# Key and query convolutions of an attention block by Strassen–Winograd products taken twice instead of once

## The chip, the cores and the metric

The kernel runs on one core of a Trainium2 chip. TensorE (PE) multiplies, VectorE (DVE), ScalarE (ACT) and GpSimd (POOL) do elementwise work, and SyncE (SP) issues nearly all DMAs. The metric is the device time of one execution in microseconds; lower is better. Everything is fp32.

## What is computed

Eight images of 512 channels and 32 x 32 = 1024 tokens pass through two attention blocks. Block 0 has a group norm of 32 groups and eight heads of 64 channels; block 1 has a group norm of 8 groups and one head of 512 channels. Cut to what matters here, block 0 is:

```python
h = group_norm(x, gn_weight, gn_bias)                       # 32 groups
qkv = einsum('oc,bct->bot', w_qkv, h) + b_qkv[None, :, None]
qkv = qkv.reshape(B * nh, 3 * C // nh, T)
q, k, v = qkv[:, :ch], qkv[:, ch:2 * ch], qkv[:, 2 * ch:]
weight = softmax(einsum('bct,bcs->bts', q * scale, k * scale))
a = einsum('bts,bcs->bct', weight, v)
out = x + einsum('oc,bct->bot', w_proj, a) + b_proj[None, :, None]
```

The change concerns the q and k of block 0: two products of a 512 x 512 matrix with the 512 x 1024 image. A bias of k adds the same number to all scores of a query, so the softmax doesn't depend on it.

## The kernel before

**One level of seven products.** Each convolution splits the weights and the image in 2 x 2 halves and makes seven products of half size in place of eight (`wino`, L226). Sums of the weights' quarters (factors 5, 6, 3, 7) are made once and kept in DRAM (`prepare`, `keep`); a convolution loads all seven factors, 1.79 MB, with `load_weight` (L298) into a pool of three tiles. The list `uses` fixes the order of these loads, and a load is issued when a convolution ends. The sums of the image's quarters (`image_factors`, L311) are 16 VectorE operations of 512 columns per image, each reading two SBUF operands.

`wino` does a product per step, on two output tiles i of 128 x 512 each. Product 1 goes to bank a, is copied by ScalarE (t1) and continued by product 2 in a. Products 6, 7 and 4 add up in bank b; product 5 and 3 in bank c. Between two of them VectorE reads the partial sum (`upper`, `done`): u2 = b + t1 after 6, u3 = b + t1 after 7, the output quarters from c and b. The last two steps stand in a list `tail`; `finish()` runs them after step 1 of the following convolution, so that there is always a product between a bank's reading and its next writing.

**Order.** TensorE's instructions, some of ScalarE's and some of VectorE's are kept in program order (`keep_in_program_order`); for the rest a scheduler orders each engine by priority. `background` is a list of small jobs (image factors, statistics of the next norm), of which each step runs some. `hooks` are jobs tied to a step.

**An image.** Attention of block 0 for image b (`attention0`, L400) has eight blocks of scores: eight tiles sc of 128 x 1024 in three PSUM tiles, ScalarE's e = exp(sc), VectorE's sums of the e, then av, the product with v. `reciprocals` (L371) takes the sums; the result is multiplied in by GpSimd. Then come block 1 of image b - 1 (`layer1_scores`, `layer1_rest`), the projection, and the convolutions for image b + 1: `queries` (q), then `keys_and_values` (k, then v). Scores of b + 1 follow directly after v. The norm of image b + 2 is made within these convolutions: statistics on VectorE from four loads `ahead`, `group_mean` (L109: one small matmul, four VectorE operations of four columns) and `affine` (L122: a small matmul, VectorE's ve, GpSimd's power rstd at L127, then VectorE's s, ms and b). `biased` (L351) writes q and k with their bias added: ScalarE for the quarter from bank a, VectorE for the others.

The prologue does the same for image 0 with the sums fresh in SBUF, and forms m (the product of block 1's query and key weights), z (of its value and projection weights) and the bias rows.

Of the kernel before, what the change touches and what calls it, by code (L numbers as in the profile page):

```python
# [9 lines left out]
F32 = mybir.dt.float32  # L10
# [4 lines left out]

P = 128
EPS = 1e-5
NBIG = 32


# [8 lines left out]
def two_attention_blocks_kernel(  # L29
# [41 lines left out]
    def pcols(name):  # L71
        i = 4 * PARAMS.index(name)
        return par[:, i : i + 4]
# [101 lines left out]
    def main_path(ctx):  # L175
# [46 lines left out]
        def finish():  # L222
            while tail:
                tail.pop(0)()
# [46 lines left out]
        wdram = {n: dram.tile([P, 7, 2, C // 2], F32, name=f"sums_{n}") for n in weights}  # L271

        def weight_factors(t):
            return {p: t[:, p - 1, :, :] for p in range(1, 8)}

        def prepare(n):
            t = wpool.tile([P, 7, 2, C // 2], F32, tag="w", name=f"prepare_{n}")
# [11 lines left out]
        def keep(n, t):  # L289
            nc.sync.dma_start(wdram[n], t)  # L290

        uses = ["q", "p", "k", "v"] if B > 1 else ["p"]
        for b in range(1, B):
            uses += ["m", "p", "z"] + (["q", "k", "v"] if b + 1 < B else [])
        uses += ["m", "z"]
        loaded = []

        def load_weight():  # L298
            if uses:
                n = uses.pop(0)  # L300
                t = wpool.tile([P, 7, 2, C // 2], F32, tag="w", name=f"w_{n}_{len(uses)}")
                nc.sync.dma_start(t, wdram[n])
                loaded.append((n, t))

        def weight(n):
            name, t = loaded.pop(0)
            assert name == n
            return weight_factors(t)


        def image_factors(h, uid):  # L311
# [53 lines left out]
        def conv(wf, hf, bias, name, **kw):  # L365
            out = channel_tiles(name)
            by_channel(wf, hf, name, biased(out, bias), **kw)
            return out


# [204 lines left out]
        def prologue():  # L575
            raw_k = raw("k", 5)
            raw_q = raw("q", 4)
            h0 = [load_x(0, c, "h0") for c in range(KC)]
            first = {n: prepare(n) for n in "vqk"}
            wk = natural(raw_k, "k", ("a", "b"))  # L580
            wq = natural(raw_q, "q", ("c", "acc"))
            norm = GroupNorm(0, "0_0", pinned=True)
            for c in range(KC):
                norm.stats(c, h0[c])
            hf, steps = image_factors(h0, "h0_0")

# [23 lines left out]
            q = conv(weight_factors(first["q"][0]), hf, pcols("bq0"), "q0_0")  # L610
            k = conv(weight_factors(first["k"][0]), hf, pcols("bk0"), "k0_0")
# [12 lines left out]
            later.append([  # L624
                lambda: tc.keep_in_program_order(nc.vector.tensor_copy(ubias, bias[0])),
                lambda: tc.keep_in_program_order(nc.vector.tensor_add(obias[1], bias[1], pcols("bp1"))),
                lambda: tc.keep_in_program_order(nc.vector.tensor_add(obias[0], bias[2], pcols("bp0"))),
            ])
            return v, q, k, norm1, later
# [56 lines left out]
                [lambda: norm.affine(acc_tile(f"gvar_{uid}")[:, :KC])],  # L686
            ]

        def keys_and_values(b, hf, hooks):

            norm = None
            if b + 1 < B:
                norm = GroupNorm(0, f"0_{b + 1}")
                for c in range(KC):
                    background.append(lambda c=c: norm.stats(c, load_x(b + 1, c, "ahead")))
            k = conv(weight("k"), hf, pcols("bk0"), f"k0_{b}", hooks=hooks, after=[load_weight])
            hooks = [[all_background], [], [], [], []]
            if norm:
                hooks[1].append(lambda: norm.group_mean(acc_tile(f"gmean_0_{b + 1}")[:, :KC]))
                hooks[3].append(lambda: norm.affine(acc_tile(f"gvar_0_{b + 1}")[:, :KC]))  # L700
            v = by_token(weight("v"), hf, f"v0_{b}", hooks=hooks, after=[load_weight])
            return k, v, norm

        def queries(b, h, hooks=()):
            hf, steps = image_factors(h, f"h0_{b}")
            background.extend(steps)
            q = conv(
                weight("q"), hf, pcols("bq0"), f"q0_{b}", middle=(2, 5, 6, 7), hooks=hooks, back=4, after=[load_weight],
            )
            return hf, q  # L710

        def layer1_scores(b, h, hooks):
            hf, steps = image_factors(h, f"h1_{b}")
# [34 lines left out]
        for b in range(B):  # L748
            extra = [[] for _ in range(2 * 2 * KC)]
            for i, fs in enumerate(later):  # L750
                extra[i] += fs
            later = []
            h, loads, applies = [], [], []
            if b > 0:
                h, loads, applies = begun(load_again, norm1, b - 1, "h1")
            elif B > 1:
                h, loads, applies = begun(load_x, norm0, 1, "h0")
            for f in loads:
                f()
            for i, f in enumerate(applies):  # L760
                extra[2 * i + 3].append(f)
            psum_pools(f"attention_{b}", 1)
            a, scaled = attention0(b, q, k, v, extra)
            psum_pools(f"products_{b}", 2)
            xt = [load_x(b, c, "x") for c in range(KC)]
            af, ends = attention_steps(a, scaled, b)
            if b > 0:
                hf, gf = layer1_scores(b - 1, h, ends)
                norm1 = projection(b, af, xt)
                if b + 1 < B:  # L770
                    h, loads, applies = begun(load_x, norm0, b + 1, "h0")
# [220 lines left out]
```

## Time and profile before

| what | value |
|---|---|
| median of 3 runs | 2933.57 us (2933.5 to 2934.69) |
| profiled execution | 2936.12 us, span 2934.3, TensorE clock 0.999 |
| DMA | 245.80 MB, mean 84 GB/s |
| VectorE adds of 128x512 from PSUM (w_k, L237) | 692 ns each, x16 |
| ScalarE's exponentials (e, L417) | 476.0 us, x512, mean 1050 ns |
| ScalarE's copies from PSUM, 128x512 (L248) | 586 ns each |
| GpSimd's multiplications a<-a,r (L438) | 104.0 us, x56 |

One profiled execution: times are microseconds from the start of the span unless marked ns. A row names line, engine, operation, output<-inputs and their shapes, count, busy time and mean. "Idle before" is the engine's own waiting time ahead of an instruction, and the arrow names what ended it. PEld is TensorE's weight load, which runs beside its products. A matmul of fp32 has two MATMUL records.

In the timeline of before, the convolutions for image 2 lie at 610 to 697 us: q, from 641 k, from 665 v; the scores begin at 696.6.

### The profile page before, as it was taken

To read this page: it belongs to the slowest core of one execution; us is meant where nothing else is said; L and a number is where in the kernel's file an instruction comes from. 1 tells how busy PE (TensorE), PEld (TensorE's weight loads), DVE (VectorE), ACT (ScalarE), POOL (GpSimd) and SP (SyncE) were. 2 spreads that over 40 slices of the span, in tenths; PEclk is the share of its full clock that TensorE was granted. 3 is DMA by queue.
4 is the path that set the end of the run, shared out by engine and by line. 5 is a ranking of instruction groups with operands and counts; after the bars stand their busy time and mean duration, and the time that the engine had idled before them with its cause. 6 is when DMAs were issued, how large, how long until landed. Compare 5 with 4: busy or idle time off the path is not lost.

```text
span 2934.3 us, 26701 instructions
## 1 busy us (share of the span) xinstructions
PE 2919.7 (100%) x10250; PEld 1390.3 (47%) x10250; DVE 1852.9 (63%) x2381; ACT 809.3 (28%) x1005; POOL 201.7 (7%) x161
## 2 busy tenths in 40 slices
PE   9999999999999999999999999999999999999999
PEld 5434534545345453454534544345543455334544
DVE  5487577555876458664686546866477653776555
ACT  1251251213512035120451104411054110531110
POOL 0010010000100001000120001100011000110000
PEclk9999999999999999999999999999999999999999
DMA  7332302222032221222212221122311222112201
GB/s 264 131 128 107 119 19 103 78 106 87 23 108 97 76 86 48 83 97 75 90 46 81 97 100 66 48 79 104 122 39 45 79 108 90 40 44 79 90 4 66
DMA packets 69676, 245.80 MB, mean 84 GB/s; under 512 B 9955, under 2 KB 16931, under 8 KB 63014
## 3 DMA queue, kind: packets, MB, share of 16 engines
q1 hardware_dynamic: 69126, 243.87, 22.9%
q8 instruction: 82, 1.34, 0.2%
q14 instruction: 52, 0.43, 0.0%
q10 hardware_dynamic: 416, 0.16, 0.0%
HBM read 197.03 MB, written 46.96 MB: 83 GB/s over the span
## 4 chain that ended last, share of the span: by engine, by line
PE 98%; DVE 1%; DMA 0%; issue 0%; ACT 0%; SPq 0%; DVEq 0%
PE sc L66 15%; PE av L66 15%; PE psb_sc L66 6%; PE psb_av L66 6%; PE psa_av L66 4%; PE psa_sc L66 4%; PE psc_av L66 4%; PE psc_sc L66 4%; PE psb_z L66 3%; PE psb_g L66 3%; PE psb_k L66 3%; PE psb_p L66 3%; PE psb_v L66 3%; PE psb_q L66 3%; PE psa_g L66 2%; PE psa_v L66 2%
## 5 line engine op out<-in xcount | busy, mean ns | idle before, releaser
L421 DVE TENSOR_TENSOR sum<-sum,e 128x1024 f32<-128x1024 f32 x384 | 519.3, 1352 | 41.4 <-DVE sum L421 0.9
L417 ACT ACTIVATE e<-sc 128x1024 f32<-128x1024 f32 x512 | 476.0, 1050 | 164.6 <-PE sc L66 164.6
L66 PE MATMUL sc<-q,k 64*128 64x512 f32 x2048 | 456.8, 596 | 0.0
L66 PE MATMUL av<-e,v 128*64 128x512 f32 x2048 | 453.6, 595 | 0.0
L66 PEld LDWEIGHTS sc<-q,k 64*128 64x128 f32 x2048 | 190.4, 186 | 239.7 <-ACT e L417 119.2
L66 PEld LDWEIGHTS av<-e,v 128*64 128x64 f32 x2048 | 141.4, 137 | 304.3 <-issue 304.3
L382 DVE RECIPROCAL rc<-sums 128x256 f32<-128x256 f32 x72 | 126.4, 1756 | 87.7 <-PE sums L66 85.4
L384 POOL TENSOR_TENSOR all_recs<-all_recs,rc 128x256 f32<-128x256 f32 x72 | 63.8, 886 | 1056.9 <-DVE rc L382 1049.3
L435 ACT COPY a<-av 128x512 f32<-128x512 f32 x64 | 37.5, 586 | 321.3 <-PE av L66 321.3
L469 ACT ACTIVATE e<-e 128x512 f32<-128x512 f32 x96 | 60.5, 630 | 232.7 <-DVE e L468 232.7
L438 POOL TENSOR_TENSOR a<-a,r 128x512 f32<-128x512 f32 x56 | 104.0, 1857 | 276.1 <-DMA r<-rows 260.0
L419 DVE TENSOR_TENSOR sum<-e,e 128x1024 f32<-128x1024 f32 x64 | 78.6, 1227 | 60.1 <-ACT e L417 60.1
L66 PE MATMUL psa_sc<-g,h 128*128 128x512 f32 x256 | 115.7, 594 | 0.0
L66 PE MATMUL psa_av<-e,z 128*128 128x512 f32 x256 | 113.3, 595 | 0.0
L127 POOL TENSOR_TENSOR rstd<-ve,mhalf 128x4 f32<-128x4 f32 x16 | 16.3, 1019 | 1204.1 <-DVE ve L125 1204.1
L139 ACT ACTIVATE h<-h,b,s 128x1024 f32<-128x1024 f32 x62 | 78.5, 1270 | 60.1 <-DMA h<-in_x 48.9
L66 PEld LDWEIGHTS psa_sc<-g,h 128*128 128x128 f32 x256 | 48.1, 190 | 57.9 <-issue 56.2
L66 PEld LDWEIGHTS psa_av<-e,z 128*128 128x128 f32 x256 | 48.0, 190 | 57.3 <-issue 55.9
L248 ACT COPY t_sc<-psa_sc 128x512 f32<-128x512 f32 x32 | 18.7, 586 | 181.7 <-DVE x L669 152.4
L66 PE MATMUL psb_sc<-g,h 128*128 128x512 f32 x128 | 58.1, 597 | 0.0
L66 PE MATMUL psa_z<-w_z,h 128*128 128x256 f32 x256 | 57.9, 379 | 0.0
L66 PE MATMUL psb_z<-w_z,t_h 128*128 128x256 f32 x256 | 57.9, 379 | 0.0
(266 smaller groups left out, 4027.7 us busy)
## 6 DMA issues: line engine op xcount, KB each, us to landing
x<-in_x SPq DMA_DIRECT2D x36, 512.0 KB
h<-in_x SPq DMA_DIRECT2D x32, 512.0 KB
r<-rows SPq DMA_DIRECT2D x128, 128.0 KB
spill<-x SPq DMA_DIRECT2D x32, 512.0 KB
h<-spill SPq DMA_DIRECT2D x32, 512.0 KB
x<-spill SPq DMA_DIRECT2D x32, 512.0 KB
out<-x SPq DMA_DIRECT2D x64, 256.0 KB
w_p<-sums_p SPq DMA_DIRECT2D x8, 1792.0 KB
```

Of the source, the lines that this page charges most:

```text
L66: tc.keep_in_program_order(nc.tensor.matmul(*args, **kw))
L127: nc.gpsimd.tensor_tensor(rstd, ve, mhalf, ALU.pow)
L139: tc.keep_in_program_order(nc.scalar.activation(dst, src, AF.Identity, bias=b, scale=s))
L248: nc.scalar.copy(t1[i], ps["a", i])
L382: nc.vector.reciprocal(rc, sums)
L384: nc.gpsimd.tensor_tensor(all_recs, all_recs, rc, ALU.add)
L417: nc.scalar.activation(e, sc, AF.Exp, scale=(C // 8) ** -0.5)
L419: nc.vector.tensor_add(total, es[0], e)
L421: nc.vector.tensor_add(total, total, e)
L435: nc.scalar.copy(dst, av)
L438: nc.gpsimd.tensor_tensor(dst, dst, r, ALU.mult)
L469: nc.scalar.activation(dst, dst, AF.Exp, scale=scale)
```

## The change

- q and k of images 1 to 7 are made by `conv2`: both levels of the split at once, 49 products of 128 x 128 weights with 256 columns of the image, where there were 7 products of twice the size in each direction. The outer products are taken in four pairs, (1,5), (2,6), (7) and (3,4); for each inner product j both outer products of a pair are made into the two halves of one bank.
- After inner product 1, ScalarE copies bank a into a bank b in PSUM, and inner products 6, 7 and 4 add to the copy. The outer sums are made while reading the banks: VectorE adds what the output already holds (`add`), and for pair 3 GpSimd adds output blocks to each other in SBUF (`more`, eight a convolution). Inner products 3 and 4 of a pair run after the next pair's product 1.
- The image's inner sums (`inner_factors`) are 28 GpSimd operations of 128 x 256 an image, in seven more tiles of the pool `big`.
- The inner sums of the weights are made once, in the prologue, by GpSimd (`keep2`, for q before and for k after image 0's convolution of k) and stored in seven pieces; a convolution loads them in two parts.
- k has no bias; q's is added by ScalarE in place, in halves (`biased_half`).
- v comes first, then k, then q. In image 1 the projection stands between v and k. Image 0 is made as before.

The diff, cut in places:

```diff
--- before.py
+++ after.py
...
+        wdram2 = {n: dram.tile([P, 7, 7, P], F32, name=f"sums2_{n}") for n in "qk"}
+        def keep2(n, t):
+            u = wpool.tile([P, 4, 7, P], F32, tag="w", name=f"prepare2_{n}")
+            quarter = lambda k, i: t[:, :, k, ts(i, P)]
+            a11, a21, a12, a22 = quarter(0, 0), quarter(0, 1), quarter(1, 0), quarter(1, 1)
+            s1, s2, s3, s4 = (u[:, i, :, :] for i in range(4))
+            for dst, x, y, op in (
+                (s1, a21, a22, ALU.add), (s2, s1, a11, ALU.subtract), (s3, a11, a21, ALU.subtract),
+                (s4, a12, s2, ALU.subtract),
+            ):
+                nc.gpsimd.tensor_tensor(dst, x, y, op)
+            for j, f in enumerate((a11, a12, s4, a22, s1, s2, s3)):
+                nc.sync.dma_start(wdram2[n][:, :, j, :], f)
+        twice = [("k", 0), ("k", 1), ("q", 0), ("q", 1)]
+        uses = ["v", "p", *twice] if B > 1 else ["p"]
         for b in range(1, B):
-            uses += ["m", "p", "z"] + (["q", "k", "v"] if b + 1 < B else [])
+            uses += ["m", "p", "z"] + (["v", *twice] if b + 1 < B else [])
         uses += ["m", "z"]
         loaded = []
         def load_weight():
             if uses:
                 n = uses.pop(0)
-                t = wpool.tile([P, 7, 2, C // 2], F32, tag="w", name=f"w_{n}_{len(uses)}")
-                nc.sync.dma_start(t, wdram[n])
+                t = wpool.tile([P, 7 * C], F32, tag="w", name=f"w_{n[0]}_{len(uses)}")
+                if n in twice:
+                    t = t.rearrange("p (i j m) -> p i j m", i=4, j=7)
+                    i = n[1]
+                    t = t[:, : 4 - i]
+                    nc.sync.dma_start(t, wdram2[n[0]][:, 4 * i : 4 + 3 * i])
+                else:
+                    t = t.rearrange("p (i k m) -> p i k m", i=7, k=2)
+                    nc.sync.dma_start(t, wdram[n])
                 loaded.append((n, t))
-        def weight(n):
+        def weight_part(n):
             name, t = loaded.pop(0)
             assert name == n
-            return weight_factors(t)
+            return t
+        def weight(n):
+            return weight_factors(weight_part(n))
...
         def conv(wf, hf, bias, name, **kw):
             out = channel_tiles(name)
             by_channel(wf, hf, name, biased(out, bias), **kw)
+            return out
+        def inner_factors(hf, uid):
+            f, steps = {}, []
+            for p in ORDER:
+                t = big_tile(f"inner{p}_{uid}", (P, 4, 2 * P))
+                t1, t2, t3, t4 = (t[:, i, :] for i in range(4))
+                b11, b12, b21, b22 = (hf[p][k][:, ts(i, 2 * P)] for k in range(2) for i in range(2))
+                f[p] = {1: b11, 2: b21, 3: b22, 4: t4, 5: t1, 6: t2, 7: t3}
+                def make(ops=((t1, b12, b11), (t2, b22, t1), (t3, b22, b12), (t4, b21, t2))):
+                    for dst, x, y in ops:
+                        nc.gpsimd.tensor_tensor(dst, x, y, ALU.subtract)
+                steps.append(make)
+            return f, steps
+        def conv2(n, f, bias, name, hooks=()):
+            out = channel_tiles(name)
+            hooks = list(hooks)
...
+            def add(dst, ps, x):
+                n = max(len(dst), len(x))
+                for i in range(n):
+                    d = dst[i] if len(dst) == n else dst[0][:, i : i + 1, :]
+                    nc.vector.tensor_add(d, ps[:, i : i + 1, :] if n > 1 else ps, x[i] if len(x) == n else x[0][:, i : i + 1, :])
+            def more(dst, x, y, r, cc):
+                (d,), (x,), (y,) = (blocks([at], r, cc) for at in (dst, x, y))
+                nc.gpsimd.tensor_tensor(d, x, y, ALU.add)
+            def biased_half(i, c):
+                if bias is not None:
+                    for r in range(2):
+                        oc = 2 * i + r
+                        t = out[oc][:, ts(c, HT)]
+                        nc.scalar.activation(t, t, AF.Identity, bias=bias[:, oc : oc + 1])
+            def pair(s, products, y, x, final):
+                w = weights2[s // 2][:, (0, 2, 0, 1)[s] :]
+                ps, tmp = {}, {}
+                k = len(products)
+                def bank(n):
+                    ps[n] = ps_pools["abc".index(n)].tile([P, 2, 2 * P], F32, tag="ps", name=f"ps{n}_{name}_{s}")[:, :k, :]
+                def keep_tmp(what, tag):
+                    tmp[what] = upool.tile([P, 2, 2 * P], F32, tag=f"{tag}{s % 2}", name=f"{what}_{name}_{s}")[:, :k, :]
+                    return tmp[what]
+                def mm(n, j, start):
+                    for i, p in enumerate(products):
+                        matmul(
+                            ps[n][:, i, :], w[:, i, j - 1, :], f[p][j], start=start and i == 0, stop=True, skip_group_check=True
+                        )
+                def step(j):
+                    if j == 1:
+                        bank("a")
+                        mm("a", 1, True)
+                        bank("b")
+                        nc.scalar.copy(ps["b"], ps["a"])
+                    elif j == 6:
+                        mm("b", 6, False)
+                        if x is None:
+                            nc.scalar.copy(keep_tmp("u2", "u"), ps["b"])
+                        else:
+                            add([keep_tmp("u2", "u")], ps["b"], blocks(x, 0, 1))
+                            extra(0, 1, True, False)
+                    elif j == 2:
+                        mm("a", 2, False)
+                        if x is None:
+                            (d,) = blocks(y, 0, 0)
+                            nc.scalar.copy(d, ps["a"])
+                        else:
+                            add(blocks(y, 0, 0), ps["a"], blocks(x, 0, 0))
+                            extra(0, 0, True, True)
+                    elif j == 5:
+                        bank("c")
+                        mm("c", 5, True)
+                        if x is None:
+                            nc.scalar.copy(keep_tmp("c5", "w"), ps["c"])
+                        else:
+                            add([keep_tmp("c5", "w")], ps["c"], blocks(x, 1, 1))
+                            extra(1, 1, True, False)
+                    elif j == 7:
+                        mm("b", 7, False)
+                        add(blocks(y, 1, 1), ps["b"], [tmp["c5"]])
+                        extra(1, 1, False, True)
+                    elif j == 3:
+                        mm("c", 3, False)
+                        add(blocks(y, 0, 1), ps["c"], [tmp["u2"]])
+                        extra(0, 1, False, True)
+                    elif j == 4:
+                        mm("b", 4, False)
+                        if x is None:
+                            (d,) = blocks(y, 1, 0)
+                            nc.scalar.copy(d, ps["b"])
+                        else:
+                            add(blocks(y, 1, 0), ps["b"], blocks(x, 1, 0))
+                            extra(1, 0, True, True)
+                    run_background(1)
+                def extra(r, cc, read, written):
+                    if products == (7,):
+                        if read:
+                            more((0, 1), (0, 1), (1, 1), r, cc)
+                        if written:
+                            more((1, 1), (1, 0), (1, 1), r, cc)
+                step(1)
+                finish()
+                for j in (6, 2, 5, 7):
+                    step(j)
+                for g in hooks.pop(0) if hooks else ():
+                    g()
+                tail.extend([lambda: step(3), lambda: step(4)])
+                tail.extend(final)
+            weights2 = [weight_part((n, 0))]
+            pair(0, (1, 5), [(1, 0), (1, 1)], None, [])
+            pair(1, (2, 6), [(0, 0), (0, 1)], [(1, 0), (1, 0)], [load_weight, lambda: biased_half(0, 0)])
+            weights2.append(weight_part((n, 1)))
+            pair(2, (7,), [(1, 0)], [(0, 1)], [lambda: biased_half(1, 1)])
+            pair(3, (3, 4), [(0, 1), (1, 0)], [(0, 1), (1, 0)], [load_weight, lambda: biased_half(0, 1), lambda: biased_half(1, 0)])
             return out
@@ -602,14 +775,15 @@
             v = by_token(weight_factors(first["v"][0]), hf, "v0_0", middle=(2, 5, 6, 7), back=4)
             finish()
             run_background(len(background))
-            for n in "vqk":
-                keep(n, first[n][0])
+            keep("v", first["v"][0])
...
             k = conv(weight_factors(first["k"][0]), hf, pcols("bk0"), "k0_0")
             finish()
+            keep2("k", first["k"][0])
...
@@ -686,28 +860,29 @@
                 [lambda: norm.affine(acc_tile(f"gvar_{uid}")[:, :KC])],
             ]
-        def keys_and_values(b, hf, hooks):
-
+        def values(b, h, hooks=()):
+            hf, steps = image_factors(h, f"h0_{b}")
+            background.extend(steps)
+            inner, steps = inner_factors(hf, f"h0_{b}")
+            background.extend(steps)
             norm = None
             if b + 1 < B:
                 norm = GroupNorm(0, f"0_{b + 1}")
                 for c in range(KC):
                     background.append(lambda c=c: norm.stats(c, load_x(b + 1, c, "ahead")))
...
+            v = by_token(weight("v"), hf, f"v0_{b}", middle=(2, 5, 6, 7), hooks=hooks, back=4, after=[load_weight])
+            return v, inner, norm
+        def keys_and_queries(b, f, norm, hooks):
+            k = conv2("k", f, None, f"k0_{b}", hooks)
+            hooks = [[all_background], [], []]
             if norm:
                 hooks[1].append(lambda: norm.group_mean(acc_tile(f"gmean_0_{b + 1}")[:, :KC]))
...
+                hooks[2].append(lambda: norm.affine(acc_tile(f"gvar_0_{b + 1}")[:, :KC]))
+            q = conv2("q", f, pcols("bq0"), f"q0_{b}", hooks)
+            return q, k
...
@@ -774,12 +949,12 @@
                 ahead = [loads, *([f] for f in applies)]
                 layer1_rest(b - 1, hf, gf, norm_hooks(norm1, f"1_{b}"), ahead)
                 if b + 1 < B:
-                    hf, q = queries(b + 1, h)
-                    k, v, norm0 = keys_and_values(b + 1, hf, ())
+                    v, f, norm0 = values(b + 1, h)
+                    q, k = keys_and_queries(b + 1, f, norm0, ())
             elif B > 1:
-                hf, q = queries(1, h, ends)
+                v, f, norm0 = values(1, h, ends)
                 norm1 = projection(0, af, xt)
-                k, v, norm0 = keys_and_values(1, hf, norm_hooks(norm1, "1_0"))
+                q, k = keys_and_queries(1, f, norm0, norm_hooks(norm1, "1_0")[1:])
             else:
                 for f in sum(ends, []):
                     f()
```

More of the change, by code (lines that the diff above doesn't have):

```diff
@@ L17 @@
 EPS = 1e-5
+ORDER = (1, 5, 2, 6, 7, 3, 4)
 NBIG = 32
@@ L273, in weight_factors @@
         def weight_factors(t):
-            return {p: t[:, p - 1, :, :] for p in range(1, 8)}
+            return {p: t[:, ORDER.index(p), :, :] for p in range(1, 8)}
         def prepare(n):
@@ L290, in keep @@
             nc.sync.dma_start(wdram[n], t)
-        uses = ["q", "p", "k", "v"] if B > 1 else ["p"]
+        wdram2 = {n: dram.tile([P, 7, 7, P], F32, name=f"sums2_{n}") for n in "qk"}
[13 more added lines that the diff above has]
+        uses = ["v", "p", *twice] if B > 1 else ["p"]
         for b in range(1, B):
-            uses += ["m", "p", "z"] + (["q", "k", "v"] if b + 1 < B else [])
+            uses += ["m", "p", "z"] + (["v", *twice] if b + 1 < B else [])
         uses += ["m", "z"]
@@ new lines, in conv2, with blocks @@
+        def conv2(n, f, bias, name, hooks=()):
+            out = channel_tiles(name)
+            hooks = list(hooks)
+            def blocks(places, r, cc):
+                if len(places) == 2 and places[0][0] == places[1][0] and places[0][1] < places[1][1]:
+                    t = out[2 * places[0][0] + r].rearrange("p (c q n) -> p c q n", c=2, q=2)
+                    return [t[:, :, cc, :]]
+                return [
+                    out[2 * i + r].rearrange("p (c q n) -> p c q n", c=2, q=2)[:, c : c + 1, cc, :] for i, c in places
+                ]
+            def add(dst, ps, x):
[92 more added lines that the diff above has]
+            pair(3, (3, 4), [(0, 1), (1, 0)], [(0, 1), (1, 0)], [load_weight, lambda: biased_half(0, 1), lambda: biased_half(1, 0)])
@@ L610, in prologue @@
             q = conv(weight_factors(first["q"][0]), hf, pcols("bq0"), "q0_0")
+            keep2("q", first["q"][0])
             k = conv(weight_factors(first["k"][0]), hf, pcols("bk0"), "k0_0")
             finish()
+            keep2("k", first["k"][0])
             norm1.group_mean(acc_tile("gmean_0_1")[:, :KC])
@@ L695, in keys_and_values @@
                     background.append(lambda c=c: norm.stats(c, load_x(b + 1, c, "ahead")))
-            k = conv(weight("k"), hf, pcols("bk0"), f"k0_{b}", hooks=hooks, after=[load_weight])
-            hooks = [[all_background], [], [], [], []]
+            v = by_token(weight("v"), hf, f"v0_{b}", middle=(2, 5, 6, 7), hooks=hooks, back=4, after=[load_weight])
[3 more added lines that the diff above has]
+            hooks = [[all_background], [], []]
             if norm:
                 hooks[1].append(lambda: norm.group_mean(acc_tile(f"gmean_0_{b + 1}")[:, :KC]))
[L700 to L710, printed above, removed]
+                hooks[2].append(lambda: norm.affine(acc_tile(f"gvar_0_{b + 1}")[:, :KC]))
+            q = conv2("q", f, pcols("bq0"), f"q0_{b}", hooks)
+            return q, k
         def layer1_scores(b, h, hooks):
```

## The prediction

> **What bounds the kernel now.** I read the page first (busy shares, chain that ended last), then windows and timelines of one image's convolutions, image 2, from about 610 to 711 us. The fences follow that order.
>
> ```profile
> PE 2919.7 (100%) x10250; PEld 1390.3 (47%) x10250; DVE 1852.9 (63%) x2381; ACT 809.3 (28%) x1005; POOL 201.7 (7%) x161
> ...
> PE 98%; DVE 1%; DMA 0%; issue 0%; ACT 0%; SPq 0%; DVEq 0%
> ```
>
> TensorE has work for 2919.7 us of a span of 2934.3, and 98% of the last chain is its own. Fewer TensorE cycles are gained one for one, as long as nobody makes TensorE wait; every new wait is lost one for one. The windows show it for the convolutions:
>
> ```profile
> core 0: us, PE busy (x) PEld busy (x) DVE busy (x) ACT busy (x) POOL busy (x), PEclk, DMA share, GB/s
> ...
> 641.00:665.00 24.00, 24.00 (x57) 10.64 (x56) 12.03 (x22) 2.55 (x4) 0.00 (x0) 1.00 0.22 77
> 665.00:696.60 31.60, 31.60 (x133) 24.58 (x131) 11.86 (x24) 2.35 (x4) 1.02 (x1) 1.00 0.33 125
> ```
>
> 641 to 665 is the key convolution without a gap: 56 records, VectorE half idle, GpSimd empty. The timeline of TensorE gives the two prices (columns: start, duration, what, count):
>
> ```profile
> 671.93 3.60 PE L66 MATMUL psc_k<-h,w_k 128*128 128x512 f32 x8
> 675.36 0.81 PE L66 MATMUL psb_v<-w_v,t_h 128*128 128x256 f32 x3
> ```
>
> A record of 512 columns takes (675.36 - 671.93)/8 = 0.429 us, one of 256 columns (0.81 - 0.38)/2 = 0.215, where 0.38 is the page's mean of a single one. Each fp32 product is two records: 0.858 and 0.4315 us. The weight load (0.19 us a record) stays below both.
>
> What a late reader of PSUM does is seen once, in image 1's query convolution:
>
> ```profile
> 252.47 0.68 DVE L237 TENSOR_TENSOR u_q<-psb_q,t_q 128x512 f32<-128x512 f32 x1
> ...
> 253.20 3.36 PE L66 MATMUL psb_q<-h,w_q 128*128 128x512 f32 x7 [1.17 <-DVE u_q L237]
> ```
>
> TensorE may add product 7 to bank b only when VectorE has read product 6 out of it. It resumes 0.05 us after that read, having lost 1.17. Usually a step has two output tiles of 1.72 us, so that the reader has a whole tile's time. Finally, what GpSimd costs and does to VectorE:
>
> ```profile
> 241.45 0.98 POOL L384 TENSOR_TENSOR all_recs<-all_recs,rc 128x256 f32<-128x256 f32 x1 [8.57 <-DVE rc L382]
> ...
> 241.76 0.94 DVE L383 TENSOR_TENSOR low_recs<-low_recs,rc 128x256 f32<-128x256 f32 x1
> ...
> 686.51 1.02 POOL L127 TENSOR_TENSOR rstd<-ve,mhalf 128x4 f32<-128x4 f32 x1 [114.97 <-DVE ve L125]
> ```
>
> The VectorE instruction, 0.424 us when alone (the least of its group), waits for the GpSimd one: both read two SBUF operands. The third line is the norm's power, 1.02 us for four columns.
>
> [...]
>
> **The change part by part**, against the profiled execution (2936.12 us; the median is 2.55 lower).
>
> *Products.* 28 x 0.858 = 24.03 us become 49 x 0.4315 = 21.14 per convolution: -2.89, for q and k of seven images (image 0 keeps the old form): 14 x 2.89 = **-40.4 us**. It is certain, since nothing else sets these stages now.
>
> *Adds in PSUM.* With two products side by side a step lasts 0.86 us, in the third pair (product 7 alone) 0.43. Reading a bank costs 0.04 to 0.1 us to start (VectorE began w_k at 663.53, 0.04 after the end of TensorE's record), 0.424 per 256 columns (period 0.44) and 0.055 back. VectorE's adds: first pair 2 of 512 columns (ScalarE copies the rest), second 8 of 256 and 2 of 512, third 6, fourth 12. The last three pairs load it with 26 x 0.44 + 2 x 0.72 = 12.9 us of 15.1. So its mean load fits, but the order does not everywhere:
> - First and second pair: slack, but product 3 of the second waits about 0.05 us for its bank.
> - Third pair: product 7 follows product 6 into bank b after two steps of 0.43; VectorE still has a backlog from the pair before. About 0.5 us lost; then product 6 of the fourth pair waits 0.1 us for ScalarE's copy of the bank (0.586 for 512 columns; some 0.4 for 256, an estimate from it).
> k: 0.05 + 0.5 + 0.1, about **0.7 us, x7 = 4.9**.
>
> *q has the next image's norm in it.* Four small VectorE operations (0.195 each) make the third pair's loss 0.75. Then s (L130 in the changed kernel) waits for the power on GpSimd, which stands behind four of the new GpSimd adds of 128x256 (0.73 each, from the group's undisturbed instances: 2.9 + 1.0 us in all). VectorE runs in order, so the fourth pair's read of product 6 stands behind s, and product 7 behind it: 1.7 us. The last two products have no next pair's product between them: 0.7. With 0.1 for the copy: **3.3 us, x6 = 19.8**; image 7 has no next norm: 1.2 (the third pair's 0.5, small waits, the tail). Together 21.0.
>
> *Start of attention.* q's bias is now added in place by ScalarE (0.69 per 512 columns, L356's row, eight an image), where before VectorE added it while reading. The last four stand after the last adds and ahead of the first exponential: it starts some 1.55 us later than the 1.24 us after the scores' start seen at 697.86. There are three score tiles, 2.6 us of products; the first must be read by 1.24 + 1.55 + 1.05 = 3.84, so TensorE waits 1.3, and ScalarE's period (0.904) is no shorter than TensorE's (0.86): **1.35 x 7 = 9.4 us**.
>
> *Inner factors.* 28 GpSimd operations of 128x256 an image: 28 x 0.73 to 0.98 = 20 to 27 us, from the time h is ready, about 586 in the timeline of before. They are first needed by k's second product, over 50 us later, as v now goes first. Hidden. They collide with VectorE's sums of h (two SBUF inputs): at most 0.3 us a v convolution, **2.1 us**. In image 1 these sums come some 1 to 1.5 us late once, and the 1.17 stall of the old q goes: 0.
>
> *Short waits.* Some five further waits per convolution come out with under 0.15 us to spare. In the score stage 32 records take 7.07 us for 32 x 0.2146 = 6.87 [...]. I charge 0.084: 14 x 5 x 0.084 = **5.9 us**; 0 if none stops it, double if all are a little later.
>
> *Loads.* Each of q and k takes two loads (1.83 and 1.38 MB for 1.79). One of 1.79 lands in 6 us (651.5 to 657.5); they are issued 17 us and more before use: 0. The new sums of the first weights are four GpSimd operations of 896 columns and seven stores each on SP's queue, before the loads of p and m that the prologue wants; done by about 101, needed at 117.3: 0, but 5 to 10 once if that is optimistic. k's bias is dropped, with its VectorE work.
>
> Sum: 2936.1 - 40.4 + 4.9 + 21.0 + 9.4 + 2.1 + 5.9 = 2939.0 profiled, 2936.5 as a median: practically the time of before.
>
> **Rivals.**
> 1. *The waits are mostly hidden.* If the scheduler's order lets s find its power ready, q costs 1.2 everywhere (-12.6), and if two of the four bias operations run under the last adds the attention start costs 0.6 (-5.3), and the short waits vanish (-5.9): 2913. For: VectorE is half idle in these stages. Against: GpSimd's order has the adds ahead of the power. With every wait hidden 2893 would be the floor; I give that nothing.
> 2. *VectorE becomes the bound in the last three pairs* (the other side). In k it has 15.1 us for 26 adds and 2 long ones, in q also eight small operations (1.6 us); it is the bound from a period of (15.1 - 1.44)/26 = 0.525 us in k, 0.464 in q. These adds write strided halves of the output, and each waits on its own semaphore. At 0.55 k loses 1.7 us, q 5.7 (1.6 plus the blocked s on top of a full engine): 7 x 1.7 + 6 x 5.7 + 2 = 48 where I had 26; with the rest as above 2959. For: 0.44 leaves q only 0.02 a period. Against: in the timeline short VectorE operations follow each other without a gap, and strided reads of PSUM (L346) cost the same 0.69.
> 3. *The change does not take effect*: were the products not fewer, nothing would fall. The order of TensorE's instructions shows 49 products of 256 columns, so no chance.
>
> **How the numbers follow.** The central case 0.5, rival 1 0.2, rival 2 0.3. The central case's sum has 43 us of waits against 40 of gain; a third of it either way gives 2922 to 2951. About 0.2% (5.9 us) is what this measurement can tell from no change. Of the central case I put 0.12 below 2927.7, 0.18 within and 0.20 above 2939.4. Faster 0.2 + 0.12 = 0.32, same 0.18, slower 0.50. The range takes in rival 1 with 5 us to spare and rival 2 with 7 (the prologue's loss): 2908 to 2966.
>
> **What would show it.** In the windows of k and q: TensorE's records of 0.215 us, 98 a convolution, span 21.8 us for k and 24.4 for q. In the waits: PE behind VectorE's adds of pairs three and four, one longest wait of 1.5 to 2 us per q, behind an s whose releaser is GpSimd; ScalarE's first e some 1.5 us later, TensorE's fourth score tile waiting for it. VectorE's 256-column adds at 0.424, GpSimd's at 0.73. A first wait for the inner factors or a weight load, or adds at 0.5 and above, would make the forecast wrong upward; an s that does not wait, downward.

## The result and the profile after

| | before | after |
|---|---|---|
| median | 2933.53 us (2933.0 to 2934.69, 4 runs) | 2916.36 us (2914.13 to 2919.64, 4 runs) |
| ratio after / before | | 0.9942, 95% interval 0.9925 to 0.9959 |
| profiled execution | 2936.12 us, span 2934.3 | 2914.43 us, span 2912.7 |

The change makes the kernel 17.2 us faster. The time lies in the forecast range of 2908 to 2966 us, but the sum of the forecast said no change, and half of the chance was put on slower, 0.32 on faster. The page after, busy shares and the chain that ended last:

```profile
PE 2891.4 (99%) x10838; PEld 1495.4 (51%) x10838; DVE 1940.7 (67%) x2661; ACT 872.3 (30%) x1117; POOL 463.0 (16%) x477
...
PE 94%; DVE 2%; issue 1%; ACT 1%; POOL 1%; DMA 0%; SPq 0%; DVEq 0%; POOLq 0%; ACTq 0%
```

TensorE still bounds the kernel, and its busy time is 28 us less (2919.7 before), but 6% of the last chain now belong to others, where it was 2%. What TensorE waits for (columns: engine, line, releaser; us in total, times, longest; the four longest rows):

```profile
engine line waited for: us in total, times, longest us
PE psb_q L67 <- DVE u_q L439: 6.5, 6, 1.1
PE tr_wk L70 <- DMA rawk<-in_w: 3.7, 1, 3.7
PE psc_q L67 <- DVE c_q L439: 1.2, 6, 0.2
PE sc L67 <- ACT e L590: 1.1, 7, 0.2
```

Six times, once per image 1 to 6, product 7 of q's last pair stands behind VectorE's read of product 6. Seven times, once per image, the scores stand behind an exponential. The view doesn't show all of a loss: the records next to a wait also start further apart than usual (q of image 2 waits for 1.08 and 0.19 us in the view and loses 2.4 by the starts). So in what follows a loss of q, k or v is counted from the starts of TensorE's records that write its tiles (`psb_q` and so on), over images 1 to 7. From each record to the start of the next, what exceeds the record's own price is loss. The prices are the usual distances of two starts in both traces: 0.429 us for 512 columns and 0.2158 for 256 (half of the 0.4315 of a product). Score records start in pairs and count 0.2146 each; their loss is over all eight images. Image 2 of the changed kernel in windows: k, then q, then the first scores.

```profile
core 0: us, PE busy (x) PEld busy (x) DVE busy (x) ACT busy (x) POOL busy (x), PEclk, DMA share, GB/s
642.90:664.40 21.50, 21.50 (x99) 18.46 (x99) 12.21 (x29) 4.41 (x8) 5.63 (x8) 1.00 0.42 151
664.40:687.40 23.00, 21.72 (x101) 17.84 (x100) 13.80 (x39) 7.00 (x12) 6.63 (x9) 1.00 0.66 251
687.40:695.00 7.60, 7.45 (x33) 2.55 (x32) 4.08 (x5) 7.60 (x11) 0.00 (x0) 1.00 0.66 243
```

k takes 21.5 us where it took 24.0; q 23.0, 1.5 more than k. VectorE is busy for 57% and 60% of them, so it isn't the bound; it is late at certain places. The timelines of VectorE and then of GpSimd (start, duration, what, count) show the place in q that the prediction spoke of, and the third fence TensorE's side:

```profile
677.26 0.41 DVE L439 TENSOR_TENSOR u_q<-psb_q,q 128x256 f32<-128x256 f32 x1
677.59 0.41 DVE L439 TENSOR_TENSOR q<-psa_q,q 128x256 f32<-128x256 f32 x1
677.92 0.41 DVE L439 TENSOR_TENSOR c_q<-psc_q,q 128x256 f32<-128x256 f32 x1
...
681.66 0.68 DVE L130 TENSOR_TENSOR s<-rstd,par 128x4 f32<-128x4 f32 x1 [2.58 <-POOL rstd L128]
...
683.32 0.75 DVE L439 TENSOR_TENSOR u_q<-psb_q,q 128x256 f32<-128x256 f32 x2
```

```profile
677.75 1.41 POOL L444 TENSOR_TENSOR q<-q,q 128x256 f32<-128x256 f32 x2 [15.85 <-DVE u_q L439]
679.24 0.72 POOL L444 TENSOR_TENSOR q<-q 128x256 f32<-128x256 f32 x1
679.93 0.72 POOL L444 TENSOR_TENSOR q<-q,q 128x256 f32<-128x256 f32 x1
680.61 1.02 POOL L128 TENSOR_TENSOR rstd<-ve,mhalf 128x4 f32<-128x4 f32 x1
```

```profile
684.12 1.13 PE L67 MATMUL psb_q<-inner_h,w_q 128*128 128x256 f32 x4 [1.08 <-DVE u_q L439]
685.44 0.70 PE L67 MATMUL psc_q<-h,w_q 128*128 128x256 f32 x2 [0.19 <-DVE c_q L439]
```

VectorE has written the power's input, ve, by 678.7, but GpSimd has four adds ahead of the power in its order, the first begun at 677.75, and delivers at 681.6. VectorE, in order, idles 2.58 us (bank c, written by 679.9, is read at 682.65, behind s), reads u_q at 683.3, and TensorE resumes at 684.1. The chain is the one predicted. The first three lines of VectorE's fence show what was not predicted: three adds of 256 columns start 0.33 us apart, though each lasts 0.41. Finally ScalarE at the start of the scores, which begin at 687.37:

```profile
687.07 2.56 ACT L451 ACTIVATE q<-q,par 128x512 f32<-128x512 f32 x4 [0.95 <-DVE q L439]
689.53 2.83 ACT L590 ACTIVATE e<-sc 128x1024 f32<-128x1024 f32 x3
```

The first exponential starts 2.16 us after the first score, where it was 1.24, because ScalarE's four bias operations of q run ahead of it.

### The profile page after: what moved, and what is told of

The parts are those of the page before. It is cut to its first block, busy times and chain, and to the rows that moved or that the text cites. A ratio compares the mean times of both kernels' runs of the same rounds, so it can differ in the third digit from the quotient of the medians.

```text
span 2912.7 us, 28999 instructions
## 1 busy us (share of the span) xinstructions
PE 2891.4 (99%) x10838; PEld 1495.4 (51%) x10838; DVE 1940.7 (67%) x2661; ACT 872.3 (30%) x1117; POOL 463.0 (16%) x477
## 4 chain that ended last, share of the span: by engine, by line
PE 94%; DVE 2%; issue 1%; ACT 1%; POOL 1%; DMA 0%; SPq 0%; DVEq 0%; POOLq 0%; ACTq 0%
PE av L67 15%; PE sc L67 15%; PE psb_sc L67 6%; PE psb_av L67 6%; PE psa_av L67 4%; PE psa_sc L67 4%; PE psc_av L67 4%; PE psc_sc L67 4%; PE psb_z L67 3%; PE psb_p L67 3%; PE psb_g L67 3%; PE psb_v L67 3%; PE psb_k L67 3%; PE psc_z L67 2%; PE psa_z L67 2%; PE psc_p L67 2%
## 5 line engine op out<-in xcount | busy, mean ns | idle before, releaser
L594 DVE TENSOR_TENSOR sum<-sum,e 128x1024 f32<-128x1024 f32 x384 | 518.9, 1351 | 40.4 <-ACT e L590 0.5
L611 POOL TENSOR_TENSOR a<-a,r 128x512 f32<-128x512 f32 x56 | 112.1, 2002 | 267.8 <-DMA r<-rows 258.3
L67 PE MATMUL psb_q<-inner_h,w_q 128*128 128x256 f32 x294 | 75.5, 385 | 6.5 <-DVE u_q L439 6.5
L67 PE MATMUL psb_k<-inner_h,w_k 128*128 128x256 f32 x294 | 75.3, 383 | 0.0
L444 POOL TENSOR_TENSOR k<-k,k 128x256 f32<-128x256 f32 x28 | 20.1, 727 | 291.1 <-DVE u_k L439 291.1
```

Source lines behind the costliest of these rows:

```text
L67: tc.keep_in_program_order(nc.tensor.matmul(*args, **kw))
L444: nc.gpsimd.tensor_tensor(d, x, y, ALU.add)
L594: nc.vector.tensor_add(total, total, e)
L611: nc.gpsimd.tensor_tensor(dst, dst, r, ALU.mult)
```

## The experiments

Each is the changed kernel with the edit shown; the diffs are cut and shortened in places (`...`). All were compared with the kernel before on the same chip; its medians there were 2933.2 to 2933.8 us.

| run | us (median, lowest to highest) | ratio to before, 95% interval |
|---|---|---|
| norm made sooner (e1) | 2905.64, 2905.10 to 2912.09 | 0.9903, 0.9887 to 0.9920 |
| q's bias in VectorE's reads (e2) | 2912.90, 2912.07 to 2913.39 | 0.9928, 0.9912 to 0.9945 |
| both (e3) | 2906.36, 2903.03 to 2908.00 | 0.9908, 0.9892 to 0.9925 |
| GpSimd's adds on VectorE (e4) | 2920.74, 2920.06 to 2924.87 | 0.9955, 0.9938 to 0.9971 |
| image 1's inner factors held back (e5) | 2917.62, 2916.02 to 2920.39 | 0.9949, 0.9936 to 0.9963 |
| v first, old products (e6) | 2935.18, 2934.43 to 2938.08 | 1.0007, 0.9999 to 1.0016 |
| k by 49 products, q as before (e7) | 2918.17, 2917.37 to 2923.36 | 0.9954, 0.9939 to 0.9970 |
| e1, e2 and e5 together (e8) | 2905.63, 2905.20 to 2906.15 | 0.9905, 0.9890 to 0.9920 |
| inner factors on VectorE (e9) | 2926.06, 2923.74 to 2928.64 | 0.9974, 0.9965 to 0.9982 |
| e3, image 1's inner factors on VectorE (e10) | 2908.05, 2907.34 to 2911.99 | 0.9918, 0.9904 to 0.9931 |

**e1: the norm's power away from the adds.**

```diff
-            hooks = [[all_background], [], []]
-                hooks[1].append(... norm.group_mean ...)
-                hooks[2].append(... norm.affine ...)
...
+                first[2] = first[2] + [all_background]        # hooks of k's pairs
+                first[3] = first[3] + [... norm.group_mean ...]
+                hooks[0].append(... norm.affine ...)          # hooks of q's pairs
...
```

> The next image's norm is made some 20 us sooner: group mean after k's fourth pair, the power and s after q's first pair, so that no GpSimd add of q stands ahead of the power. Theory A (s waiting for the power behind four adds is what image 1 to 6's q loses): q of images 1 to 6 falls from 2.47 us of TensorE waits to the 0.8 of image 7, 6 x 1.65 = 10 us less, about 2906 us (profiled about 2904.5). Rival B (the loss is VectorE's backlog in pairs three and four, and s only stands in it): q keeps 1.8 us or more, and the time falls by under 4 us. Rival C (the wait moves into q's first pair): a new TensorE wait of about 1 us near q's start, and no gain.

Measured: 2905.64 us. q's loss over the seven images falls from 14.9 to 5.9 us; image 2's q falls from 2.4 to 0.9 us, near the 0.7 of image 7, which has no next norm. The timeline of VectorE and GpSimd in image 2:

```profile
675.07 0.16 DVE L130 TENSOR_TENSOR s<-rstd,par 128x4 f32<-128x4 f32 x1 [1.13 <-POOL rstd L128]
```

```profile
674.02 1.02 POOL L128 TENSOR_TENSOR rstd<-ve,mhalf 128x4 f32<-128x4 f32 x1 [7.31 <-DVE ve L126]
682.77 1.42 POOL L444 TENSOR_TENSOR q<-q,q 128x256 f32<-128x256 f32 x2 [7.74 <-DVE u_q L439]
```

VectorE still waits 1.13 us for the power, but in q's first pair, where no product waits for what stands behind it. By product, the fourth pair's product 7 loses 1.35 us in image 2 of the changed kernel and nothing in e1; the third pair's product 7 loses 0.22 in both, though e1 also takes the four small operations of `group_mean` away from it. So nearly all of the gain goes with the power. Theory A holds in place and in size; B and C fall.

**e2: the bias of q.** In the three pairs after the first, the read that makes a final block adds its bias; the in-place operations go.

```diff
-                    nc.vector.tensor_add(d, ps..., x...)
...
+                    if bias is not None and r is not None and oc is not None:
+                        nc.vector.scalar_tensor_tensor(d, a, bias[:, oc + r : oc + r + 1], y, ALU.add, ALU.add)
+                    else:
+                        nc.vector.tensor_add(d, a, y)
...
-            ... [load_weight, lambda: biased_half(0, 1), lambda: biased_half(1, 0)])
+            ... [load_weight])
```

> q's bias is added by VectorE in reads that it makes anyway (scalar_tensor_tensor of 128x256 in place of add, 12 a convolution), and the eight ScalarE operations an image are gone. Theory A (the four bias operations ahead of the first e make TensorE wait at the attention's start): e_0 starts 1.24 us after the scores' start as before the change, the score stage's excess falls by 6 us in all, q's stalls stay: about 2910 us. Rival B (the score stage waits for VectorE's last reads of the banks): the first scores still wait some 0.9 us an image and nothing is gained. Rival C (the scalar_tensor_tensor is dearer than the add by 0.06 us or more and lengthens VectorE's chain): q gains stalls of 0.5 us, half of the gain is lost.

Measured: 2912.90 us. In image 2 the first exponential starts 1.23 us after the first score, as before the change. The score stage's loss falls from 18.9 to 14.8 us (12.8 before the change): theory A is right, but 4.1 us come back where it said 6. In image 2 a part of the rest is rival B's wait: VectorE's last add of q ends at 688.43, and the weight loads of the next scores, which wait for it, start at 688.55. q's loss rises from 14.9 to 17.3: theory C is right as well. The new operation takes 0.477 us where the add takes 0.415. By the stages the net gain is 1.7 us; the medians say 3.5, with a changed kernel that itself spreads over 5.5 us.

e2 also measures how sensitive q is to VectorE's price: 12 operations of 0.062 us more, 0.74 in all, cost (17.3 - 14.9)/7 = 0.34 us of TensorE's time per q.

**e3: both.**

> Both edits of e1 and e2. If the two waits are separate, the gains add: some 16 us, about 2900 us. If both sit on the same chain (VectorE late at q's end delays the bias and the first scores too), the gain is that of the larger alone, 2904 to 2908.

Measured: 2906.36 us, lowest 2903.03. ScalarE goes straight to the exponentials; the scores begin at 684.6:

```profile
685.81 4.85 ACT L595 ACTIVATE e<-sc 128x1024 f32<-128x1024 f32 x5 [7.04 <-PE sc L67]
```

By the stages q loses 7.2 us and the scores 14.8, together 2.8 less than in e1 (5.9 and 18.9); by the medians there is no difference between the two. The two waits are separate by the stages, but what the bias adds is smaller than the spread.

**e4: GpSimd's adds on VectorE**, `nc.gpsimd.tensor_tensor` in `more` replaced by `nc.vector.tensor_tensor`.

> The eight GpSimd adds of 128x256 per convolution in pair three go to VectorE. Theory A (the power waits behind these adds): the power starts at once, s waits only 1.1 us; but VectorE gets 8 x 0.42 = 3.4 us more in a stretch of 9 us that it fills to 70%, so k loses about 1 us more and q changes little: between -5 and +8 us, 2911 to 2924. If GpSimd's adds were the whole cause, q of images 1 to 6 would fall to 1.2 us of waits.

Measured: 2920.74 us. q's loss hardly changes (15.5 us), k's more than doubles (2.5 to 6.5). The power now starts as soon as ve is there, but ve itself is late, behind the adds in VectorE's queue:

```profile
685.25 0.15 DVE L126 TENSOR_SCALAR ve<-gvar 128x4 f32<-128x4 f32 x1
...
686.70 0.16 DVE L130 TENSOR_TENSOR s<-rstd,par 128x4 f32<-128x4 f32 x1 [0.91 <-POOL rstd L128]
```

So it isn't GpSimd's slowness alone that makes s late: adds in front of it do so on either engine.

**e6 and e7: which part brings the gain.** e6 takes the old `conv` for k and q, with v first. e7 takes `conv2` for k and `conv` for q.

```diff
-            k = conv2("k", f, None, f"k0_{b}", hooks)        # e6 only
+            k = conv(weight("k"), hf, pcols("bk0"), f"k0_{b}", hooks=[[]] + list(hooks), after=[load_weight])
-            q = conv2("q", f, pcols("bq0"), f"q0_{b}", hooks)
+            q = conv(weight("q"), hf, pcols("bq0"), f"q0_{b}", hooks=hooks, after=[load_weight])
...
```

> Only the order of the change: v first, then k, then q, both by seven products as before, no inner factors, no second weight sums, biases as before. If the order alone did something (it takes the 1.17 us stall of image 1 away, and moves VectorE's statistics), it gives 2930 to 2934. Theory: 2932, so that 49 products for 64 with all their waits bring some 16 to 18 us.

> k by 49 products as in the change, q by seven products of twice the size with its bias added in the reads, v first. Theory A (q's form pays for itself hardly: 21.14 + 2.47 us of waits + 0.87 at the attention's start against 24.04): k alone gives nearly the whole gain, 2932 - 7 x 2.42 = 2915 us, equal to the changed kernel. Rival B (q's waits are partly there with the old form too, because the norm and the bias sit there): k alone gives half, 2922 to 2926.

Measured: the order alone gives 2935.18 us, no gain (the 1.2 us wait in image 1's q goes and a 1.8 us wait in its v comes). k alone gives 2918.17 us, as good as the changed kernel within its spread. So in the change as it was made k brings nearly everything; q's 20.2 us of fewer products are spent on 13.3 us more of its own waits (14.9 for 1.6) and 6.1 at the start of the scores. Theory A holds, 3 us off in its time.

**e5, e9, e10 and e8: GpSimd and image 1.** Executions of the changed kernel lie up to 5.5 us apart. The profile of e1 is of its slowest execution, and has this in image 1 (timeline of VectorE, then of TensorE):

```profile
256.54 6.07 DVE L170 TENSOR_TENSOR t_a<-a 128x512 f32<-128x512 f32 x1
```

```profile
268.24 5.39 PE L67 MATMUL psb_p<-t_a,w_p 128*128 128x512 f32 x8 [2.73 <-DVE v L375]
```

One VectorE operation with two SBUF inputs lasts 6.07 us, from 256.5 to 262.6, while GpSimd runs eight inner factors end to end; in the changed kernel's profile the same operation took 1.24. TensorE then waits for VectorE. The windows of e1 show a second loss right after (its 0.57 is the granted clock):

```profile
258.00:268.00 10.00, 7.51 (x34) 6.08 (x32) 10.00 (x13) 0.59 (x1) 5.11 (x7) 1.00 0.15 37
268.00:272.00 4.00, 3.77 (x5) 1.65 (x6) 4.00 (x8) 0.00 (x0) 0.00 (x0) 0.57 0.61 255
```

With the mean granted clock at 0.57, the eight records of `psb_p` take 5.39 us, where eight of that shape took 3.60 in the trace of before. The two cost 2.9 and 1.8 us. e4's profile, also of its slowest execution, shows the same (6.04 us, and a mean clock of 0.58 from 266 to 270). Three kernels take image 1's factors out of the way: e5 by a copy of one column of t_a into each factor tile ahead of its sums, e9 by VectorE for all images, e10 by VectorE for image 1 on top of e3; e8 is e3 with e5's copy.

> Changed kernel; only in image 1 the inner factors on GpSimd are held back (a copy of one column out of the last VectorE sum of the attention's result, t_a, into each of their tiles) until that sum is written, so that they no longer run back to back beside it. Theory A (in some executions one t_a of VectorE stands 6 us behind a chain of GpSimd operations, and TensorE then loses 4.7 us in image 1's v and projection): the stall is gone from every execution, the times lie within 1.5 us of each other, at about 2914. Rival B (the spread of 2914 to 2920 comes from the loads of the prologue): the times still spread over 4 us or more.

> Changed kernel with the 28 inner factors of each image on VectorE in place of GpSimd. Theory A (VectorE is busy 12 of 32 us beside v and has room for 28 x 0.34 = 9.5 us; the only visible effect of GpSimd is image 1's blocked t_a): v's waits stay under 0.5 us an image, k and q as in the changed kernel, times of 2913 to 2917 without the outlier at 2919. Rival B (the inner sums stand ahead of v's reads of PSUM in VectorE's order): v loses 1 to 2 us an image, 2921 to 2930, and GpSimd was needed.

> As e3 (norm sooner, q's bias in VectorE's reads), with the inner factors of image 1 alone on VectorE. If the blocked t_a is what spreads e3's times (2903.0 to 2908.0): all times within 1 us of 2903.5. If VectorE's 9.5 us more make v or the projection of image 1 wait: one loss of 1 to 3 us, all times near 2905 to 2906, as e8. If the spread comes from elsewhere: still over 3 us between runs.

> Changed kernel with the norm made sooner (as in e1), q's bias in VectorE's reads (as in e2) and image 1's inner factors held back (as in e5). If these are three separate waits: 2902 to 2904 us in every execution, the fastest of all. If the held-back factors come late for k of image 1: one wait of 1 to 4 us there, and 2905 to 2907.

Measured: e5's times still lie 4.4 us apart and e10's 4.7, so the blocked operation isn't the whole of the spread. In e5's profile the operation lasts 0.64 us, but v loses 1.8 us more in image 1, because VectorE now has the statistics and t_a ahead of u_v. e8 loses 2.7 us more in the same place, and gives 2905.2 to 2906.2 in all its runs. e9 costs 9.7 us: v's loss rises from 0.4 to 9.6 us over the seven images, 0.8 in image 2 and 5.7 in image 1, and the clock takes 3 us more after image 1's waits (its mean is 0.56 from 269.9 to 277). Rival B of e9 holds in the time, if not image by image, so GpSimd is needed for the factors, though it is not free. None of the four beats e1 or e3 clearly.

The mean granted clock of every execution is on record, and in e9 and e10, whose profiles have waits of 2 and 3 us in image 1, the spread goes with it. Of e9's twelve executions three at 1.000 took 2923.7 to 2924.4 us, three at 0.999 took 2925.2 to 2925.9, six at 0.998 took 2926.2 to 2928.6; e10's five stand in the same order, from 2907.3 at 1.000 to 2912.0 at 0.998. That is what a clock that falls in some executions and not in others would give (4 us at 0.57, as in e1, are 1.7 us of clock), but only one execution of each has a trace. e5's five are all at 0.999; what spreads them stays open.

## Why the prediction was wrong

Its direction was wrong because the sum of waits was twice too large: 43.3 us, where 20.4 were measured. The big waits were found where they had been put; the short waits and v's collisions weren't. On the profiled executions, in us over all images, the change from before to after:

| term of the sum | predicted | measured |
|---|---|---|
| fewer products | -40.4 | -40.4 (0.858 and 0.4315 a product) |
| k's waits | +4.9 | +2.4 |
| q's and v's waits | +21.0 + 2.1 | +11.9 |
| start of the scores | +9.4 | +6.1 |
| short waits | +5.9 | 0 beyond the above |
| prologue, other stages | 0 | -1.6 |
| sum | +2.9 | -21.6 |

(The measured sum is that of the two spans. q and v go together, since the norm's small matmuls moved from v into q with the new order. Of the 22.9 us that were too many, 6.1 are q's, 5.1 v's and the old stall's in image 1, 2.5 k's, 3.3 the scores', 5.9 the short waits'.)

- **The step that failed is the spacing of VectorE's adds, "period 0.44".** It was taken from the 0.424 that one such operation lasts. In the changed kernel two of them last 0.76 and three start 0.33 apart, so that 26 a convolution are 2.8 us less than reckoned. What that is worth is an estimate. In q, by e2's slope (0.34 us of TensorE for 0.74 of VectorE), it is 1.3 us, 9 over the seven. In k, by e4's (eight adds more, 2.7 us, cost (6.5 - 2.5)/7 = 0.57), it is 0.6 us, 4 over the seven. That is 13 us where q and k together were 8.6 too dear, so the spacing is enough to account for them; no run varied it alone. Per q of image 2 the parts came out as: third pair's product 7, 0.22 for 0.75; the copy 0.06 for 0.1; the fourth pair's product 7, 1.35 for 1.7; the tail 0.46 for 0.7.

  The trace of before already had the spacing. One such `t_h` lasts 0.69 us, but two last 1.28, so that the second starts 0.08 before the end of the first; `o`, which needs `w_av`, starts 0.04 after its end:

```profile
593.02 1.28 DVE L169 TENSOR_TENSOR t_h<-h 128x512 f32<-128x512 f32 x2
...
610.31 0.69 DVE L237 TENSOR_TENSOR w_av<-psb_av,t_av 128x512 f32<-128x512 f32 x1 [0.50 <-PE psb_av L66]
611.04 0.69 DVE L508 TENSOR_TENSOR o<-psc_av,w_av 128x512 f32<-128x512 f32 x1
```

  In that whole trace 942 VectorE operations start 0.08 to 0.09 us before the end of the one ahead, and 426 start 0.03 to 0.04 after it, all of these on a tile of the name just written. With 0.08 off, the 0.424 would have been a period of 0.34.
- **The blocked s was right in place and near in size**, and e1 shows it: 9.0 us go with it, where the prediction had 2.1 x 6 = 12.6 as the part that goes with the power.
- **The start of the scores was right in kind**: 0.92 us later for 1.55. ScalarE's four operations follow each other 0.62 us apart in place of 0.69, and the last two adds take 0.76 for 0.88; these make 0.4 us of it, and the rest isn't accounted for. e2 and e3 take away 4.1 of the 6.1 us.
- **"Short waits", 5.9 us, were not there.** The 0.084 us charged for each was the author's estimate. In the trace of before, the 0.20 us by which a score stage exceeds its products stand in two places: 0.10 in its first pair of records and 0.10 in its last. k has 0.35 us of loss in image 2 in all, every wait included, and 0.22 of it is the third pair's product 7.
- **v and the inner factors**: hidden from image 2 on, and the collisions cost less than the 0.3 us an image allowed (v of image 2 loses 0.05 us, where it lost 0.3 before; the sums of h are eight VectorE operations an image in the trace, not sixteen). The 0 for image 1 holds for the profiled execution. In e1's and e4's profiles the collision costs 4.7 us; whether it does so in the slower executions of the changed kernel isn't shown, as they have no profile. The gain is 17.2 us by the medians and 21.7 by the profiles, because the profiled execution lies 2.6 us above the median before and 1.9 below it after.
- **Loads and prologue**: hidden, as said. (The first of the two loads, 1.83 MB, is no larger than the old one: both are 1792 KB.) The prologue even was 2 us shorter in the profile of after, of which the waits for its first loads make 0.9.
- **The rival "VectorE becomes the bound" falls**: its adds come at 0.33, far from the 0.46 and 0.525 from which it would decide. The rival "waits mostly hidden" (2913) came nearest in time, but for the wrong reason: s did wait.

## What to carry to other kernels

Where a kernel is bound by one engine and a change trades its work for many short operations elsewhere, take their spacing from a place where that engine runs several in a row, and not their duration. Look there whether each needs the result of the one before: here that made the difference between 0.08 us less than the duration and 0.04 more. After the arithmetic has been cut, look at what stands in the in-order queues at the seam between the new stages: here a normalisation of four columns and four bias operations took back 15 of 40 us, and moving the first by 20 us in the program gave back 9. Try each half of a change alone: q's half brought next to nothing until its norm was moved.

## What the runs showed of the hardware that was not expected

- VectorE's adds of 128x256 out of PSUM last 0.41 us and start 0.33 us apart in the changed kernel; with two SBUF inputs (e4) the same, 0.41 and 0.33. In the trace of before, operations that need the one before them start 0.03 to 0.04 us after its end instead.
- A VectorE operation with two SBUF inputs lasted 6.07 us in e1 and 6.04 in e4, while GpSimd ran eight operations in a row, and 1.24 us in the changed kernel's profile. VectorE's adds with one input in PSUM didn't get longer beside GpSimd there: `k<-psa_k,k` took 0.418 us beside one of its operations (21 times) and 0.420 alone (14 times).
- After TensorE had waited 2.7 us (e1, e4) and 3.0 us (e9), the mean granted clock was 0.57 and 0.58 over some 4 us, and 0.56 over some 7; after a wait of 3.0 us in e10 it was 1.00 from 258 to 285. Six waits of 1.1 us in the changed kernel left it at 1.00. So with waits of 3.0 us the clock fell in one execution and not in another; no run varied the wait alone.
